# A scan kernel's prologue, written anew in halves of tokens and chunks of channels

## The chip, the cores and the metric

The kernel runs on one core of a Trainium2 chip. A core has five engines that work side by side: TensorE (PE, matrix products), VectorE (DVE), ScalarE (ACT, activation functions), GpSimd (POOL) and SyncE (SP, which here only issues DMA transfers). Each engine takes its own instructions strictly in order; semaphores make one wait for another. The metric is the time on the device in microseconds (us): the median of three runs. The profile is of one further execution.

## The reference, cut to what matters

The input x is 8 batches of 512 tokens by 256 channels, in fp32. Four layers are added to it one after the other: a Mamba block (layer a), a gated recurrence over the batches (layer b), an attention with 16 heads (c), and the recurrence once more (d). All of the change lies in the opening of layer a:

```python
h = layernorm(layernorm0(x), ln1_g, ln1_b)
y = rmsnorm(h, rms_w)
xi, z = split(y @ in_proj_w)                  # 256 channels each
xc = silu(causal_conv4(xi) + conv_b)
dbc = xc @ x_proj_w                           # 64 + 16 + 16 columns
delta = softplus(dbc[..., :64] @ dt_proj_w + dt_proj_b)
Bm, Cm = dbc[..., 64:80], dbc[..., 80:96]
# for every channel and each of 16 states, along the tokens:
#   s = exp(delta * A) * s + delta * xc * Bm ;  y = sum(s * Cm)
...
h = h + ((y + D * xc) * silu(z)) @ out_proj_w
x = x + h ; x = x + ffn(layernorm(x))
```

## The kernel before, in words

**Tiling.** 512 tokens by 256 channels are held either with tokens on the 128 partitions (4 token chunks of 256 channels, TC) or with channels on the partitions (2 channel chunks, KC, of 512 tokens). The scan works on 32 units for each batch; a unit is 8 channels times 16 states, 128 rows of 512 tokens, and two units make a pair, so a batch has 16 pairs. Units 0 to 15 are channel chunk 0, and units 16 to 31 chunk 1.

**The way of a batch to the scan** (`mamba_in`). Layer norm: `stats` on DVE and POOL (the power -0.5 runs on POOL, L82), `center` on ACT (L108), `affine` (L186, L187), `square` on ACT (L193, each with a read of its accumulator), `rms`, `outer` (ACT) and `residual` (the part that is added back later, L204), `scale` (ACT, L208). Then `turn` (PE, transposes) and `turn_` (ACT), `proj` (PE), `proj_` (ACT) and `conv` (DVE, L243), the two Silu pieces, `xproj` (PE) and its copy `xproj_` (ACT), which also stores the B and C rows to DRAM; `dt` (PE) and `dt_` (ACT), and the softplus: `soft_exp` (Exp and two Identity on ACT), `soft_rest` (two subtractions), `soft_ln` (Ln on ACT), `soft` (two DVE operations that give dl, which is delta, and dx, which is delta times xc). `side` is DVE for batch 0 and POOL for the others: it runs `affine`, `residual` and `soft_rest`. Last, `store_dl` and `store_dx` write dl and dx to DRAM, 512 KB each.

**The scan loop.** A unit's rows of dl and dx are loaded back from DRAM by SP, each row to 16 partitions (`load_unit`, L361, 256 KB each). `decay` is an Exp on ACT from dl into one of three PSUM tiles (L368), `increments` a product on POOL for each pair (bx, L375), and `scan_pair` runs two scans (L384) and two products (L388) on DVE. The tiles of loaded rows are pairs, three for dx and three for dl, so dx of pair 3 is loaded when the increments of pair 0 have been made.

**The order.** All of it is written out by hand: `manual_schedule` keeps each engine's instructions in the order of the program. `FRONT` is the list that runs first. In it `i` is batch 0 and `e` is batch 1, whose opening pieces (`stats` to `square`) also belong to the front. Behind FRONT stand the loads of the first pairs in one loop over the units 0 to 7 (dx of all eight, dl of the first six), the increments of pairs 0 and 1, and the decays of units 0 to 2. Then come 16 slots for each batch (`SLOTS`): in slot n the scan of pair n, decays, increments and loads ahead of it, and between them pieces of the next batch (`i`), of the one after that (`e`) and of the one before (`o`, `r`, `q`). The first two slots begin

```python
da0 y a.take_c bx i.rms i.scale scan q.g0 o.gate1 i.turn1 i.turn0 ld q.i0_ q.g0_ i.turn1_ da1 i.turn0_
da0 scan q.update0 da1 ld o.proj0 o.proj1 i.proj0 bx
```

where `i` is by now batch 1 (its `rms` waits for its `square`, which is in the front), `bx` makes the increments of the pair two ahead, `da0` and `da1` the decays of the third and fourth unit after the pair's first, and `ld` loads dx four pairs ahead and dl three ahead.

**PSUM.** Products and transposes of `mamba_in` use three tiles with the tag "mm" in turn; one is free again when its last reader has run.

Of the kernel before, what the change touches and what calls it, by code (L numbers as in the profile page):

```python
# [9 lines left out]
F32 = mybir.dt.float32  # L10
# [5 lines left out]
P = 128  # L16
B = 8
L = 512
# [6 lines left out]
QR = 4  # L25
KCONV = 4
# [35 lines left out]
def token_stats(cx, x, name):  # L62

    nc = cx.nc
    st = cx.small.tile([P, TC, 6], F32, tag="st", name=f"st_{name}")
    mv = cx.small.tile([P, TC, 2], F32, tag="mv", name=f"mv_{name}")
    for c in range(TC):
        nc.vector.bn_stats(st[:, c, :], x[:, c, :])
    for c in range(TC):
        nc.vector.bn_aggr(mv[:, c, :], st[:, c, :])  # L70
    return mv


def inv_sqrt(cx, v, scales, name):

    nc = cx.nc
    n = len(scales)
    ve = cx.small.tile([P, n, TC], F32, tag=f"ve{n}", name=f"ve_{name}")
    r = cx.small.tile([P, n, TC], F32, tag=f"rs{n}", name=f"rs_{name}")
    for i, (scale, eps) in enumerate(scales):  # L80
        nc.vector.tensor_scalar(ve[:, i, :], v, scale, eps, ALU.mult, ALU.add)  # L81
    nc.gpsimd.tensor_tensor(  # L82
        r.rearrange("p n c -> p (n c)"),
        ve.rearrange("p n c -> p (n c)"),
        cx.neg_half[:, : n * TC],
        ALU.pow,
    )
    return r


def layernorm_scales(cx, x, name, scales=((1.0, EPS),)):

    nc = cx.nc
    mv = token_stats(cx, x, name)
    neg = cx.small.tile([P, TC], F32, tag="neg", name=f"neg_{name}")
    nc.vector.tensor_scalar_mul(neg, mv[:, :, 0], -1.0)
    r = inv_sqrt(cx, mv[:, :, 1], scales, name)
    nb = cx.small.tile([P, len(scales), TC], F32, tag=f"nb{len(scales)}", name=f"nb_{name}")
    for i in range(len(scales)):
        nc.gpsimd.tensor_mul(nb[:, i, :], neg, r[:, i, :])  # L100
    return [(r[:, i, :], nb[:, i, :]) for i in range(len(scales))]


def normalize(cx, out, x, scales):

    r, nb = scales
    for c in range(TC):
# [5 lines left out]
def to_channels(cx, src, k, tag, name, bufs=None):  # L113

    ps = cx.psum.tile([P, L], F32, tag=tag, name=name, bufs=bufs)
    for c in range(TC):
        cx.nc.tensor.transpose(ps[:, ts(c, P)], src[:, c, ts(k, P)], cx.ident)  # L117
    return ps

# [48 lines left out]
def mamba_in(cx, a, t, b):  # L168
# [12 lines left out]
    def center():  # L181
        t.h = cx.tok.tile([P, TC, E], F32, tag="hh", bufs=1, name=f"h_{n}")
        normalize(cx, t.h, t.x, t.inner)

    def affine():
        side.tensor_mul(t.h, t.h, cx.rows3["ln1_g"])  # L186
        side.tensor_add(t.h, t.h, cx.rows3["ln1_b"])  # L187

    def square():
        t.ms = cx.small.tile([P, TC], F32, tag="ms", name=f"ms_{n}")  # L190
        sq = cx.ch.tile([P, E], F32, tag="sq", bufs=1, name=f"sq_{n}")
        for c in range(TC):
            nc.scalar.activation(sq, t.h[:, c, :], AF.Square, accum_out=t.ms[:, c : c + 1])  # L193
# [12 lines left out]
    def scale():  # L206
        for c in range(TC):
            nc.scalar.activation(  # L208
                t.h[:, c, :], t.h[:, c, :], AF.Copy, scale=t.rms[:, 0, c : c + 1]
            )  # L210
        t.hT = cx.ch.tile([P, KC, L], F32, tag="T", bufs=3, name=f"hT_{n}")
# [91 lines left out]
    def soft_exp():  # L303

        t.w = cx.tok.tile([P, KC, L], F32, tag="h", name=f"w_{n}")
        nc.scalar.activation(t.e, t.e, AF.Exp, scale=-1.0)
        nc.scalar.activation(t.w, t.e, AF.Identity, bias=cx.one)
        nc.scalar.activation(t.w, t.w, AF.Identity, bias=cx.minus)

    def soft_rest():  # L310
        side.tensor_sub(t.e, t.w, t.e)
        side.tensor_sub(t.dl, t.dl, t.e)

    def soft_ln():
        nc.scalar.activation(t.w, t.w, AF.Ln, bias=cx.one)

    def soft():
        nc.vector.tensor_add(t.dl, t.dl, t.w)
        t.dx = cx.ch.tile([P, KC, L], F32, tag="dx", bufs=1, name=f"dx_{n}")
        nc.vector.tensor_mul(t.dx, t.dl, t.xc)  # L320

    def store(what):
        d = cx.dram.tile([KC, P, L], F32, tag=what, name=f"{what}_dram_{n}")
        nc.sync.dma_start(d.rearrange("k p l -> p k l"), getattr(t, what))
        setattr(t, what + "_d", d)
# [3 lines left out]
        for f in (  # L329
            stats, center, affine, square, rms, outer, residual, scale, silu_z, silu_x, xproj,  # L330
            xproj_, rows, take_c, soft_exp, soft_rest, soft_ln, soft,
        )
    }
    for what in ("dl", "dx"):
        pieces[f"store_{what}"] = lambda what=what: store(what)
# [44 lines left out]
def scan_pair(cx, t, b, pair):  # L380
    units = (2 * pair, 2 * pair + 1)
    for u in units:
        t.hc[u] = cx.scan.tile([P, L], F32, tag="hc", bufs=8, name=f"hc_a{b}_{u}")
# [22 lines left out]
def mamba_out(cx, a, t, b):  # L406
# [26 lines left out]
    def add_proj():  # L433
        for c0, ps in t.proj.items():
            nc.vector.tensor_add(t.u[:, c0 : c0 + 2, :], t.u[:, c0 : c0 + 2, :], ps)
# [4 lines left out]
    def residual():  # L440
        nc.gpsimd.tensor_add(t.x, t.x, t.u)

    def stats():
        t.scales = layernorm_scales(cx, t.u, n)

    def norm():
        t.un = cx.tok.tile([P, TC, E], F32, tag="h", name=f"un_{n}")
        normalize(cx, t.un, t.u, t.scales[0])
        t.h2 = cx.ch.tile([P, KC, L], F32, tag="T", bufs=3, name=f"h2_{n}")

    def turn(k):
        t.ps["h2", k] = to_channels(cx, t.un, k, "mm", f"ps_h2_{n}_{k}")

    def turn_(k):
        nc.scalar.activation(
            t.h2[:, k, :],
            t.ps["h2", k],
# [48 lines left out]
    t.proj, t.down = {}, {}  # L506
    pieces = {f.__name__: f for f in (add_proj, bias, residual, stats, norm)}
# [934 lines left out]
```

## Time and profile before

| what | value |
|---|---|
| median of 3 runs | 1666.32 us (1663.48 to 1667.64) |
| the profiled execution | 1665.1 us, its span 1663.3 us |
| mean granted TensorE clock | 0.944 of full speed |
| busy share of the span | PE 89%, DVE 70%, ACT 53%, POOL 32% |
| first scan starts | 69.91 us |
| first DVE instruction of the loops of batches 1, 2, 3 (L301) | 151.90, 235.60, 323.34 us |
| loaded rows (dx, dl), 256 KB each | 256 and 256 transfers, median 6.4 us from issue to landing |
| store of dx of batch 0, 512 KB | issued 59.02, landed 2.89 us later |

The span is from the first instruction to the last; the execution's own time has 1.8 us more around it. A line of the profile gives a start, a length, the engine, the line of the kernel, the operation, its tiles (with buffer numbers left out) and, in brackets, how long the engine had been idle before it and what released it. "x4" merges four instructions. SPq and ACTq are DMA issues on these queues. An ACT_TABLE_LOAD brings in the table of another activation function.

### The profile page before, as it was taken

What the parts mean: (1) busy time and instruction counts of PE and PEld (TensorE: products, weight loads), DVE (VectorE), ACT (ScalarE), POOL (GpSimd) and SP (SyncE); (2) the same over time, 40 slices, a digit from 0 to 9 for tenths busy, and PEclk for the clock granted to TensorE, in tenths of its full rate; (3) what the DMA queues carried; (4) which work ended last, traced back from release to release, by engine and by line L of the source; (5) the groups of instructions that cost most, each with busy time, mean ns of one, the idle gap of its engine ahead of it and who ended that gap; (6) DMA issues with size and microseconds to landing.
All of it is one profiled execution on the core that took longest, in us unless ns stands there. A gap on an engine that the chain in (4) does not pass through costs nothing.

```text
span 1663.3 us, 19592 instructions
## 1 busy us (share of the span) xinstructions
PE 1487.2 (89%) x6756; PEld 700.3 (42%) x6756; DVE 1169.9 (70%) x1643; ACT 884.3 (53%) x1323; POOL 529.9 (32%) x307
## 2 busy tenths in 40 slices
PE   2155989999999999998878999999999999999998
PEld 1012544546464646465542333333333333333346
DVE  3398998999989898972136777666676667665435
ACT  4465867677777766542223545454544545454522
POOL 3358685858686765633100000000000000000000
PEclk9575999999999999998988999999999999999999
DMA  5697988797979797950210111101010110100023
GB/s 191 160 251 205 248 214 216 219 245 210 260 207 250 198 241 200 256 128 13 67 51 25 33 27 30 34 27 33 18 39 21 38 26 26 26 8 25 28 93 126
DMA packets 110403, 196.02 MB, mean 118 GB/s; under 512 B 16448, under 2 KB 25984, under 8 KB 110304
## 3 DMA queue, kind: packets, MB, share of 16 engines
q1 hardware_dynamic: 107648, 186.61, 43.1%
q10 hardware_dynamic: 1824, 5.15, 0.9%
q0 software_dynamic: 832, 3.02, 0.5%
q8 instruction: 53, 0.87, 0.2%
q14 instruction: 46, 0.38, 0.1%
HBM read 159.06 MB, written 23.07 MB: 109 GB/s over the span
## 4 chain that ended last, share of the span: by engine, by line
PE 67%; DVE 19%; ACT 5%; DMA 4%; issue 3%; POOL 2%; SPq 1%; DVEq 0%; ACTq 0%; POOLq 0%
PE ps_s_c L1014 10%; PE ps_e_c L1014 9%; DVE hc_a L384 8%; PE ps_o_c L1060 8%; PE ps_f_o L470 5%; PE ps_f_o L494 4%; DVE hc_a L388 3%; PE ps_in_a L225 2%; PE ps_v_c L988 2%; PE ps_w_c L1101 2%; PE ps_f_d L543 2%; PE ps_i_d L543 2%; PE ps_g_d L543 2%; PE ps_f_d L552 2%; PE y_a L397 2%
## 5 line engine op out<-in xcount | busy, mean ns | idle before, releaser
L1025 DVE TENSOR_REDUCE mp<-ps_s_c 128x2 f32<-128x1024 f32 x256 | 301.9, 1221 | 183.0 <-PE ps_s_c L1014 182.6
L375 POOL TENSOR_TENSOR bx_a<-dx_rep_a,B_a 128x1024 f32<-128x1024 f32 x128 | 301.9, 2369 | 117.0 <-DVE hc_a L384 54.6
L1051 ACT ACTIVATE e_c<-ps_e_c 128x1024 f32<-128x1024 f32 x256 | 248.9, 1021 | 155.2 <-PE ps_e_c L1014 152.3
L384 DVE TENSOR_TENSOR_SCAN hc_a<-da_a,bx_a 128x512 f32<-128x512 f32 x256 | 298.5, 1206 | 18.9 <-POOL bx_a L375 11.3
L368 ACT ACTIVATE da_a<-dl_rep_a,neg_a 128x512 f32<-128x512 f32 x256 | 173.5, 688 | 135.7 <-DVE hc_a L384 91.7
L1014 PE MATMUL ps_s_c<-keys,q_c 32*128 32x512 f32 x1024 | 184.1, 646 | 2.2 <-ACT e_c L1051 1.7
L1014 PE MATMUL ps_e_c<-q_c,keys 32*128 32x512 f32 x1024 | 169.1, 644 | 3.7 <-DVE mp L1025 3.7
L388 DVE TENSOR_TENSOR hc_a<-hc_a,Cp_a 128x512 f32<-128x512 f32 x256 | 161.0, 669 | 0.0
L1060 PE MATMUL ps_o_c<-e_c,va 128*32 128x512 f32 x1024 | 138.9, 608 | 0.4 <-ACT oT_c L1076 0.3
L470 PE MATMUL ps_f_o<-h_o,w 128*128 128x256 f32 x512 | 121.7, 388 | 0.4 <-ACT f_o L483 0.4
L494 PE MATMUL ps_f_o<-w,f_o 128*128 128x256 f32 x512 | 114.2, 381 | 3.9 <-ACT f_o L483 3.9
L82 POOL TENSOR_TENSOR rs_d<-ve_d,neg_half 128x4 f32<-128x4 f32 x8 | 8.1, 1016 | 342.2 <-DVE ve_d L81 342.2
L397 PE MATMUL y_a<-hc_a,sum 128*32 128x512 f32 x512 | 92.0, 699 | 23.9 <-DVE hc_a L388 15.5
L470 PEld LDWEIGHTS ps_f_o<-h_o,w 128*128 128x128 f32 x512 | 97.3, 193 | 35.2 <-issue 12.2
L494 PEld LDWEIGHTS ps_f_o<-w,f_o 128*128 128x128 f32 x512 | 96.4, 190 | 23.1 <-ACT f_o L483 5.6
L82 POOL TENSOR_TENSOR rs_c<-ve_c,neg_half 128x4 f32<-128x4 f32 x8 | 8.1, 1014 | 301.5 <-DVE ve_c L81 301.5
L1014 PEld LDWEIGHTS ps_s_c<-keys,q_c 32*128 32x128 f32 x1024 | 59.0, 184 | 99.7 <-issue 38.5
L1014 PEld LDWEIGHTS ps_e_c<-q_c,keys 32*128 32x128 f32 x1024 | 51.6, 185 | 101.2 <-issue 67.3
L483 ACT ACTIVATE f_o<-ps_f_o,vecs 128x256 f32<-128x256 f32 x128 | 52.5, 469 | 33.7 <-PE ps_f_o L470 30.9
L117 PE MATMUL ps_hT_a<-ident,h_a 128*128 128x128 f32 x64 | 12.8, 339 | 63.1 <-ACT h_a L208 63.1
L225 PE MATMUL ps_in_a<-hT_a,w_in 128*128 128x512 f32 x128 | 68.1, 671 | 1.1 <-ACT hT_a L220 1.1
L1060 PEld LDWEIGHTS ps_o_c<-e_c,va 128*32 128x32 f32 x1024 | 20.4, 108 | 92.4 <-issue 82.6
(220 smaller groups left out, 2154.5 us busy)
## 6 DMA issues: line engine op xcount, KB each, us to landing
dx_rep_a<-dx_dram_a SPq DMA_DIRECT2D x256, 256.0 KB, 6.4
dl_rep_a<-dl_dram_a SPq DMA_DIRECT2D x256, 256.0 KB, 6.4
x<-in_x_dram SPq DMA_DIRECT2D x8, 512.0 KB, 9.2
dl_dram_a<-dl_a SPq DMA_DIRECT2D x8, 512.0 KB, 6.1
dx_dram_a<-dx_a SPq DMA_DIRECT2D x8, 512.0 KB, 3.1
pre_dram_b<-pre_b ACTq DMA_DIRECT2D x8, 512.0 KB, 5.1
pre_back<-pre_dram_b SPq DMA_DIRECT2D x8, 512.0 KB, 3.3
keys<-xT_c SPq DMA_DIRECT2D x128, 32.0 KB, 1.9
```

Source lines behind the costliest of these rows:

```text
L225: nc.tensor.matmul(ps, a.in_proj[:, k, ts(m, P)], t.hT[:, k, :], start=(k == 0), stop=(k == KC - 1))
L368: cx.nc.scalar.activation(t.da[u], t.dl_rep[u // 2][:, u % 2, :], AF.Exp, scale=a.A[:, u : u + 1])
L375: cx.nc.gpsimd.tensor_mul(t.bx[pair], t.dx_rep[pair], t.B.unsqueeze(1).to_broadcast([P, 2, L]))
L384: cx.nc.vector.tensor_tensor_scan(t.hc[u], t.da[u], t.bx[pair][:, u % 2, :], 0.0, ALU.mult, ALU.add)
L388: cx.nc.vector.tensor_mul(t.hc[u], t.hc[u], t.Cp)
L397: cx.nc.tensor.matmul(t.y[k][head(j), :], a.sum[:, r, :], t.hc[4 * quad + j], start=(r == 0), stop=(r == QR - 1),)
L470: nc.tensor.matmul(ps[:, m, :], a.w1[:, k, ts(m0 + m, P)], t.h2[:, k, ts(half, L // 2)], start=(k == 0), stop=(k == KC - 1),)
L494: nc.tensor.matmul(ps, t.f[:, m, ts(c % 2, P)], a.w2[:, m, :], start=(m == 0), stop=(m == FC - 1),)
L1014: cx.nc.tensor.matmul(ps[:, i, :], lhs[rows, :], rhs[rows, :], start=True, stop=True)
L1025: cx.nc.vector.tensor_reduce(c.mp[:, t, h : h + 2, DH], ps, AX.X, ALU.max, negate=True)
L1051: cx.nc.scalar.activation(e, ps, AF.Exp)
L1060: cx.nc.tensor.matmul(po[head(j), :], c.va[b % 2][:, t, g * HG + j, :], es[j // 2][:, j % 2, :], start=(t == 0), stop=(t == TC - 1),)
```

## The change

The pieces are cut. `center`, `affine`, `square` and `scale` can be had in halves of the tokens (".a" is token chunks 0 and 1, ".b" 2 and 3), and `silu_x`, `soft_exp`, `soft_rest`, `soft_ln`, `soft`, `store_dl` and `store_dx` in chunks of the channels (".0", ".1"). Each stays available whole, and the slots of the loop, which are not changed, use it whole, so batches 1 to 7 run the instructions that they ran. The front uses the cut pieces for batch 0 (`i`), and the loads, increments and decays of the first pairs become part of its list: `dl0` loads both units of pair 0, `bx0` makes its increments, `da0` is the decay of unit 0. The number of rows loaded is the same. e.stats stands behind i.rms, e.outer and e.center at other places, silu_z and proj2, proj3 near the end.

```diff
+    def center(half):
+        if not half:
+            t.h = cx.tok.tile([P, TC, E], F32, tag="hh", bufs=1, name=f"h_{n}")
+        cs = part_of(half)[2]
+        r, nb = t.inner
+        normalize(cx, t.h[:, cs, :], t.x[:, cs, :], (r[:, cs], nb[:, cs]))
...
+    def silu_xk(k):
+        nc.scalar.activation(t.xc[:, k, :], t.xc[:, k, :], AF.Silu)
+
+    def soft_exp(k):
+
+        if not k:
+            t.w = cx.tok.tile([P, KC, L], F32, tag="h", name=f"w_{n}")
+        e, w = (x[:, chunk(k), :] for x in (t.e, t.w))
+        nc.scalar.activation(e, e, AF.Exp, scale=-1.0)
+        nc.scalar.activation(w, e, AF.Identity, bias=cx.one)
+        nc.scalar.activation(w, w, AF.Identity, bias=cx.minus)
...
+    def soft(k):
+        if not k:
+            t.dx = cx.ch.tile([P, KC, L], F32, tag="dx", bufs=1, name=f"dx_{n}")
+        dl, w, dx, xc = (x[:, chunk(k), :] for x in (t.dl, t.w, t.dx, t.xc))
+        nc.vector.tensor_add(dl, dl, w)
+        nc.vector.tensor_mul(dx, dl, xc)
+
+    def store(what, k):
+        if not k:
+            d = cx.dram.tile([KC, P, L], F32, tag=what, name=f"{what}_dram_{n}")
+            setattr(t, what + "_d", d)
+        to, x = (
+            y[:, chunk(k), :]
+            for y in (getattr(t, what + "_d").rearrange("k p l -> p k l"), getattr(t, what))
+        )
+        nc.sync.dma_start(to, x)
...
 FRONT = """
-i.stats e.stats i.center i.affine i.square i.outer i.rms i.residual i.scale i.turn0 i.turn0_
-i.turn1 i.turn1_ i.proj0 i.proj0_ i.proj1 i.proj1_ i.conv0 i.conv1 e.center e.outer i.proj2 i.proj3
-i.silu_z i.silu_x i.xproj i.xproj_ e.affine i.dt0 i.dt0_ i.dt1 i.dt1_ i.rows i.soft_exp i.soft_rest
-i.soft_ln i.soft i.store_dl i.store_dx e.square e.residual
+i.stats i.center.a i.center.b i.outer i.affine.a i.affine.b i.square.a i.square.b i.residual i.rms
+e.stats i.scale.a i.scale.b i.turn0 i.turn1 i.turn0_ i.turn1_ i.proj0 i.proj0_ i.proj1 i.conv0
+i.proj1_ i.silu_x.0 i.conv1 i.silu_x.1 i.xproj e.center i.xproj_ i.dt0 i.dt0_ i.soft_exp.0
+i.soft_rest.0 i.soft_ln.0 e.outer i.soft.0 i.dt1 i.rows i.store_dl.0 i.dt1_ i.soft_exp.1
+i.store_dx.0 dl0 i.proj3 i.proj2 e.affine dx0 i.soft_rest.1 e.residual i.soft_ln.1 dl1 i.soft.1 da0
+dx1 dx2 e.square bx0 i.store_dl.1 da1 i.silu_z bx1 dl2 da2 i.store_dx.1 dx3
 """
...
     for one in FRONT.split():
-        piece(-1, one)
-    for u in range(8):
-        for what in ("dx", "dl"):
-            if what == "dx" or u < 6:
+        what, n = one[:-1], int(one[-1]) if one[-1].isdigit() else None
+        if "." in one:
+            piece(-1, one)
+        elif what == "bx":
+            increments(cx, T[0], 0, n)
+        elif what == "da":
+            decay(cx, a, T[0], 0, n)
+        else:
+            for u in (2 * n, 2 * n + 1):
                 load_unit(cx, T[0], 0, u, what)
-    for pair in range(2):
-        increments(cx, T[0], 0, pair)
-    for u in range(3):
-        decay(cx, a, T[0], 0, u)
```

The recurrence (`recurrent_step`) and the output pieces of `mamba_out` are also written so that they could be had in halves, but are only used whole (`for half in (None,)`), with the instructions that they had.

## The prediction, made before the run

> **What bounds the kernel now.** First the page's slices, 41.6 us each: VectorE (DVE), TensorE's granted clock and the share of the DMA engines.
>
> ```profile
> DVE  3398998999989898972136777666676667665435
> ...
> PEclk9575999999999999998988999999999999999999
> DMA  5697988797979797950210111101010110100023
> ```
>
> From the third slice to the seventeenth DVE is busy throughout: the scan loop, eight batches. Only the first two slices are thin, and the change is there. Second, the chain that ended last, cut to 0 to 160 us (start, length, what):
>
> ```profile
> 1.77 12.90 DMA x<-in_x_dram
> ...
> 17.87 1.14 DVE h_a L186
> ...
> 22.51 1.97 ACT u_a L108 x4
> 24.50 1.24 DVE u_a L204
> ...
> 59.02 2.89 DMA dx_dram_a<-dx_a
> ...
> 78.66 1.03 POOL rs_a_r L82
> 79.71 0.52 ACT h_a L208
> ...
> 84.47 7.25 DMA dl_rep_a<-dl_dram_a
> 91.76 0.04 issue
> 91.81 0.69 ACT da_a L368
> 92.50 0.70 ACT xc_a L232
> ```
>
> See where it leaves batch 0's own work: it goes through batch 1's x (landed 14.67, needed only by e.stats), through `outer` and `residual` ahead of `scale`, and at 84.47 through the replicated loads. Third, the order of time at the points I measure from:
>
> ```profile
> 25.82 1.71 ACT L208 ACTIVATE h_a<-h_a,rs_a_r 128x256 f32<-128x256 f32 x4 [1.35 <-DVE u_a L204]
> ...
> 49.18 1.28 ACT L306 ACT_TABLE_LOAD   x1
> 50.47 1.06 ACT L306 ACTIVATE e_a<-e_a 128x1024 f32<-128x1024 f32 x1
> ...
> 69.91 2.34 DVE L384 TENSOR_TENSOR_SCAN hc_a<-da_a,bx_a 128x512 f32<-128x512 f32 x2 [10.24 <-POOL bx_a L375]
> ...
> 83.36 2.34 DVE L384 TENSOR_TENSOR_SCAN hc_a<-da_a,bx_a 128x512 f32<-128x512 f32 x2 [5.36 <-ACT da_a L368]
> ```
>
> The first scan starts at 69.91, the third pair at 83.36; from 83.36 to the first instruction of batch 1's loop (151.90) DVE idles only some 5 us. So what is gained in front of the loop moves all that follows, unless a queue in the ramp takes some back. Nothing later hangs on the clock on the wall: the weights and x of batches 0 to 4 are in by about 27 us.
>
> **The change, part by part.** The code for batches 1 to 7 runs the same instructions in the same order; only the front differs. I follow it in absolute time.
>
> *To scale.* `center` starts at 9.96 as before; its two halves and `outer` follow on ACT (2.07 and 2.06) to 14.0. DVE meanwhile does `affine` in four half pieces. The 128x1024 one takes 1.22; for half I take 0.65, between 0.61 (half of it) and 0.67 (the 128x512 multiply L388). From 11.1 they end at 13.7, so they are hidden under `outer`. e.stats, which had held `affine` until 17.79, now stands behind i.rms. The four `square` with their accumulator reads take 2.13 (20.38 to 22.51), so to 16.1; ve 0.2 and pow 1.0 with the handovers give `scale` at 17.4, against 25.82: **8.4 gained**. The `residual` (1.23) runs from 14.0 and is off the path. The four L159 reductions (1.24) belong to no list; wherever they fall between 7.7 and 24 DVE has room.
>
> *To the first stores.* From scale on I keep the trace's distances: proj0_ 5.95 after it (23.35), conv0 ending at 26.45, conv1 at 28.7. The Silu table load lies under conv0; silu_x.0 is done at 27.8, silu_x.1 at 29.4. (Before, e.center, e.outer, silu_z and a joint silu_x stood on ACT from 34.17 to 41.55.) xproj's first half runs under conv1, its second (1.66, at the slow clock of the trace, 0.61) under e.center, which is 2.06 on ACT to 31.45. Then xproj_ 0.58, dt0 and its handover 1.22, dt0_ 1.27: 34.5. Table load 1.29. Exp and two Identity on 128x512 cost 2.15: the 128x1024 rows are 1.06 and 1.15, the half rows lie near 0.69 (L368). Load 1.29, Ln 0.73: 40.0, with soft_rest.0 (1.3) beneath the load. soft.0 adds 0.65: store_dl.0 is issued at 40.7, store_dx.0 at 41.4. A store of 512 KB landed in 2.89, the 64 KB one in 1.6; 256 KB lies between, I take 2.2. So the first replicated load is issued at 42.95, against 61.93: **19.0 gained**.
>
> *The ACT queue after that.* e.outer 2.06, dt1_ 1.27, load 1.29, exp.1 2.15, load 1.29, ln.1 0.73, load 1.29, da0 0.7, e.square 2.16, da1 0.7, load 1.29, silu_z 1.09, load 1.29, da2 and da3 0.7 each: from 40.0 to 58.7. There are eight table loads where there were four. i.rms of batch 1 now waits on DVE for e.square (52.95), and the first scan is queued behind it: 53.2, against 69.91 (16.7 gained). Pair 1 waits for da2: 58.05, against 74.48 (16.4).
>
> *The replicated loads.* Before, the first landed 3.4 after its issue, at 65.3, and the 25th (dl of unit 10, the one in the chain) at 91.72: 1.10 each, an unbroken stream of 256 KB. Now the first lands at 46.35 and the tenth (dx2) at 56.25. bx0 and bx1 (2.35 each) run from 49.7 and 54.1, bx2 from 56.45 to 58.8; batch 1's pow, queued behind it on POOL, is done at 59.85. ACT is free at 58.7, so POOL sets batch 1's `scale`: 59.9. Pair 2 began 3.65 after scale, so 63.5, against 83.36: 19.9 gained. Then the stream takes over: up to dl of unit 10 there are the same 24 intervals (26.5) and the two chunk-1 stores between them. A store's share of the stream no row shows alone; it is over nothing and at most a load's 1.10, I take 0.65. 46.35 + 26.5 + 1.3 = 74.2, against 91.72: **17.5 gained**. SP's waits don't starve the stream: dx3 waits for bx0 (52), dx4 for bx1 (56.5), dx6 for bx3 (about 64), each with several loads outstanding. da of unit 10 stands before proj1_, then come conv1 and pair 4 (3.74 later): 77.9 for 95.46. From there on DVE is full, and 17.5 stays.
>
> Unknowns: if the DRAM tile is tracked whole, store_dl.1 waits for dl0 and dl1 to land (about 52), and store_dx.1 for dx2 (56.3); the stream gets a hole worth 1.4 in all; if by chunk, 0. proj2 and proj3 hold two PSUM buffers until silu_z (56.0), before the transposes at 60 want them: 0; were silu_z over 4 late, scale's transposes would be late by the rest. e.affine (4.7) and e.residual on POOL end at about 44.5, 5 before bx0. POOL's bx0 overlaps soft.1 on DVE by 1; a DVE add beside POOL is seen at 2.55 instead of 1.23 (L318), so at most 1.3 on chunk 1, which has slack.
>
> **A rule against it.** The new order switches between Exp, Ln and Silu four more times. The row: a load starts at 49.18, the Exp behind it at 50.47, so a switch is 1.29. The Trainium skill, "ScalarE: Activation LUTs", section "What ACT_TABLE_LOAD costs", gives about 1.28 for the load plus 1.38 of drain, 2.66 per switch, and its section on table sets says to batch by set. By the rule seven loads on the way to da3 would each be 1.37 longer, 9.6 in all: scale at 68.3, pair 2 at 71.9, **11.5** gained. I take the row, since the wait ahead of the Exp shows no drain, and keep 11.5 for the range.
>
> **The sum.** The profiled execution took 1665.1 (span 1663.3): 1665.1 - 17.5 = 1647.6. The median shown is 1.2 above it: **1649**.
>
> **The rivals.**
> 1. *The loads don't bind* and pair 2's 19.9 stays: 1646.4. For: DVE waited only 0.7 for proj1_ at 93.23, so a little slack frees it. Against: DMA is at its limit between 60 and 100 us.
> 2. *Less arrives* (dear switches, a hole in the stream, half-size pieces dearer than taken): about 11.5 gained, 1655. For: ACT has no gap from 33 to 58. Against: the load rows.
> 3. *The loop gives it back*: no change, 1666. Against: nothing behind the front has a fixed date.
> 4. *Slower.* In the loop DVE waits for the Ln on ACT (L315) each batch, 3.96 and 3.88 us in the first two. If the new phase between ACT and DVE on entry made it longer in every batch, 8 batches at 4 more are 32: 1649 + 32 = 1681; it decides from 2.2 per batch. For: ACT comes in late. Against: the order within the loop is untouched, and the batches repeat within 83.7 to 87.7 from the copy L301 to the next.
>
> **How the numbers follow.** The forecast itself (15.5 to 19.5 gained) 0.50, rival 1 0.20, rival 2 0.20, rival 3 0.03, rival 4 0.07. This kernel's measurement can tell about 0.3%, 5 us, from no change. Faster 0.90, same 0.03, slower 0.07. The forecast's own range is 1647 to 1651; with rival 1 (down to 23 gained) and rival 2 (up to 10 gained) it is 1643 to 1657, leaving out rivals 3 and 4 and the tails.
>
> **What would show it.** After: `scale` of batch 0 near 17.4; the first store near 40.7; eight table loads of 1.28 before the first loop; the first scan near 53, pair 2 near 63.5, pair 4 near 78; the copy L301 of batch 1 near 134; periods as before. I am wrong if switches show 2.7 from end to start, if pair 4 comes after 84 with earlier dates kept (stream), or if L301's periods grow.

## The result, and the profile after

The changed kernel takes **1647.88 us** (median of 4 runs, 1642.94 to 1649.03), and the kernel before, measured beside it, 1666.59 us (4 runs, 1663.48 to 1667.64). The ratio is 0.9885, with a 95% interval of 0.9861 to 0.9909: faster by 18.7 us. The profiled executions took 1647.11 and 1665.1 us, 18.0 apart.

The page's slices of the kernel after, 41.1 us each, one digit for each:

```profile
span 1645.3 us, 19612 instructions
...
DVE  3699998989899989951156777675675767656435
...
PEclk8656989999999999999988999999999999999999
DMA  6989897989989787920211111101010110100123
```

The second slice of VectorE (DVE) went from 3 to 6 tenths. From the third to the seventeenth the row is as full as it was, so the gain lies in front of the scan loop.

The chain that ended last, of the kernel after (start, length, what), from batch 0's scale to the fifth pair of scans:

```profile
16.89 0.52 ACT h_a L221
...
32.06 2.09 PE ps_dt_a L298 x2
...
54.17 1.28 ACT L269
...
57.86 0.32 ACT da_a L408
58.18 7.01 DMA dl_rep_a<-dl_dram_a
...
65.27 0.56 ACT da_a L408
65.83 7.76 DMA dl_rep_a<-dl_dram_a
...
73.68 0.69 ACT da_a L408
74.37 0.71 ACT xc_a L247
75.10 0.76 DVE xc_a L258
...
77.34 2.34 DVE hc_a L424 x2
```

Batch 1's x and `residual` are gone from it; `outer` still lies in it, on ACT ahead of `square`. It runs through batch 0's own work, then from 34 to 58 us through ScalarE (ACT) almost without a gap, and from 58.18 through two replicated loads. The second of these is dl of unit 10. It landed at 73.60, and the decay of unit 10 at 73.68 is followed by proj1_ of batch 1 (74.37, L247), its conv (L258) and the fifth pair. In the kernel before the same link stood at 84.47 to 92.50.

The order of time in the kernel after (start, length, engine, line, operation, tiles, and in brackets the idle time before it with what ended it):

```profile
16.89 1.71 ACT L221 ACTIVATE h_a<-h_a,rs_a_r 128x256 f32<-128x256 f32 x4 [1.33 <-POOL rs_a_r L84]
...
26.54 1.28 ACT L319 ACT_TABLE_LOAD   x1 [0.71 <-DVE xc_a L258]
27.83 0.63 ACT L319 ACTIVATE xc_a<-xc_a 128x512 f32<-128x512 f32 x1
...
34.17 0.69 ACT L303 ACTIVATE dl_a<-ps_dt_a,vecs 128x512 f32<-128x512 f32 x1 [2.16 <-PE ps_dt_a L298]
...
41.67 0.35 SPq L354 DMA_DIRECT2D dl_dram_a<-dl_a  x1
43.72 1.18 SPq L401 DMA_DIRECT2D dl_rep_a<-dl_dram_a  x2
...
53.68 2.33 DVE L424 TENSOR_TENSOR_SCAN hc_a<-da_a,bx_a 128x512 f32<-128x512 f32 x2
...
63.85 2.34 DVE L424 TENSOR_TENSOR_SCAN hc_a<-da_a,bx_a 128x512 f32<-128x512 f32 x2 [1.69 <-ACT da_a L408]
...
110.79 2.54 DVE L343 TENSOR_TENSOR dl_a<-dl_a,w_a 128x1024 f32<-128x1024 f32 x1 [3.96 <-ACT w_a L337]
...
133.76 0.69 DVE L316 COPY Cp_a<-C_a 128x512 f32<-128x512 f32 x1
```

Batch 0's scale starts at 16.89 (25.82 before), the first scan at 53.68 (69.91), the third pair, which the prediction calls pair 2, at 63.85 (83.36), the fifth pair at 77.34 (95.46), and the copy that opens batch 1's loop at 133.76 (151.90). So 18.1 us are won at the fifth pair and 18.1 at batch 1's loop. The copies of the later batches stay 16.2 to 17.6 earlier (the last of them 651.20 against 668.74), and layer b's first product into ps_cu_b starts at 828.92 against 846.87, 17.95 earlier. DVE's wait for the Ln of batch 1 is 3.96, as it was; in the kernel before:

```profile
95.46 2.33 DVE L384 TENSOR_TENSOR_SCAN hc_a<-da_a,bx_a 128x512 f32<-128x512 f32 x2
...
128.91 2.55 DVE L318 TENSOR_TENSOR dl_a<-dl_a,w_a 128x1024 f32<-128x1024 f32 x1 [3.96 <-ACT w_a L315]
```

Nothing is given back.

### The profile page after: what moved, and what is told of

Its sections match the earlier page's. It is cut to its first block, busy times and chain, and to the rows that moved or that the text cites. A ratio compares the mean times of both kernels' runs of the same rounds, so it can differ in the third digit from the quotient of the medians.

```text
span 1645.3 us, 19612 instructions
## 1 busy us (share of the span) xinstructions
PE 1489.6 (91%) x6756; PEld 700.2 (43%) x6756; DVE 1171.5 (71%) x1649; ACT 890.8 (54%) x1332; POOL 529.9 (32%) x307
## 4 chain that ended last, share of the span: by engine, by line
PE 68%; DVE 18%; ACT 5%; DMA 4%; issue 3%; POOL 2%; SPq 0%; DVEq 0%; ACTq 0%; POOLq 0%
PE ps_s_c L1079 10%; PE ps_e_c L1079 9%; DVE hc_a L424 8%; PE ps_o_c L1125 8%; PE ps_f_o L518 6%; PE ps_f_o L542 5%; DMA dl_rep_a<-dl_dram_a 4%; DVE hc_a L428 4%; PE ps_v_c L1053 2%; PE ps_w_c L1166 2%; PE ps_f_d L595 2%; PE ps_i_d L595 2%; PE ps_f_d L604 2%; PE ps_g_d L595 2%; PE y_a L437 2%
## 5 line engine op out<-in xcount | busy, mean ns | idle before, releaser
L415 POOL TENSOR_TENSOR bx_a<-dx_rep_a,B_a 128x1024 f32<-128x1024 f32 x128 | 302.4, 2374 | 98.4 <-DVE hc_a L424 55.4
L552 DVE TENSOR_TENSOR x<-x,ps_f_o 128x256 f32<-128x256 f32 x32 | 13.4, 417 | 61.3 <-PE ps_f_o L542 61.0
```

Of the source, the lines that this page charges most:

```text
L415: cx.nc.gpsimd.tensor_mul(t.bx[pair], t.dx_rep[pair], t.B.unsqueeze(1).to_broadcast([P, 2, L]))
```

## The experiments

Five theories stand in the expectations. **S**: what the fifth pair waits for is the stream of replicated loads, through the decay of unit 10, which stands in ACT's queue ahead of proj1_ of batch 1. **Rival 1**: the loads don't bind, and batch 1's scale sets the fifth pair. **Rival 2**: ACT's table loads set it. **Rival 3**: the loop gives it back. **Rival 4**: the loop's wait for the Ln grows. The last expectation adds a **Rival 5**. All edits are made on the kernel after. "Fifth pair" is the start of its two scans; since the inputs land at slightly different times in each execution, I also give it from the issue of the first store. In the kernel after that is 77.34 - 41.67 = 35.67.

### Each half of the change alone

The first kernel has the halves of tokens up to `scale` and then the old order, whole pieces and all loads behind. The second has whole pieces up to `scale` and then the new order.

```diff
 i.stats i.center.a i.center.b i.outer i.affine.a i.affine.b i.square.a i.square.b i.residual i.rms
-e.stats i.scale.a i.scale.b i.turn0 i.turn1 i.turn0_ i.turn1_ i.proj0 i.proj0_ i.proj1 i.conv0
-i.proj1_ i.silu_x.0 i.conv1 i.silu_x.1 i.xproj e.center i.xproj_ i.dt0 i.dt0_ i.soft_exp.0
...
+e.stats i.scale.a i.scale.b i.turn0 i.turn0_
+i.turn1 i.turn1_ i.proj0 i.proj0_ i.proj1 i.proj1_ i.conv0 i.conv1 e.center e.outer i.proj2 i.proj3
+i.silu_z i.silu_x i.xproj i.xproj_ e.affine i.dt0 i.dt0_ i.dt1 i.dt1_ i.rows i.soft_exp i.soft_rest
+i.soft_ln i.soft i.store_dl i.store_dx e.square e.residual
+old
...
+        if one == "old":
+            for u in range(8):
...
```

> The new list up to scale.b (halves of tokens, e.stats behind i.rms), and from the first transpose on the old list with the whole pieces and the old loop of loads. Theory S (whatever brings the first replicated load forward moves all that follows by as much): scale starts at 16.9 as in the changed kernel, so everything behind it comes 8.9 us earlier than in the kernel before: dl stored near 48.9, first load 53.0, third pair of scans 74.4, fifth pair 86.5, time 1657.7. Rival (the two parts share one limit): this part alone gives less than 5 us, 1662 or more.

```diff
-i.stats i.center.a i.center.b i.outer i.affine.a i.affine.b i.square.a i.square.b i.residual i.rms
-e.stats i.scale.a i.scale.b i.turn0 i.turn1 i.turn0_ i.turn1_ i.proj0 i.proj0_ i.proj1 i.conv0
+i.stats e.stats i.center i.affine i.square i.outer i.rms i.residual i.scale
+i.turn0 i.turn1 i.turn0_ i.turn1_ i.proj0 i.proj0_ i.proj1 i.conv0
```

> The old list up to scale, and from the first transpose on the new one (chunks of channels, loads between them). Theory S: scale at 25.8 as before, then the new kernel's distances: first chunk of dl stored near 50.6, first load 52.6, fifth pair of scans 86.3, time 1656.8; the gains of the two halves of the change (8.9 and 9.8) add up to the whole. Rival (one limit shared): this part alone gives nearly the whole 18, or nearly nothing.

The halves of tokens alone take 1657.19 us (ratio 0.9952, 0.9936 to 0.9967), 7.8 less than before; the first store was issued at 50.48 and the fifth pair began at 86.32. The chunks of channels alone take 1655.84 (0.9942, 0.9925 to 0.9958), 9.2 less (both against 1665.02, the kernel before beside them); first store at 49.63, fifth pair at 85.40. Both came within a microsecond of the expected time (1657.7 and 1656.8). Together the two save 17.0 us by their medians, where the whole change saves 18.7. By the copy that opens batch 1's loop they are 9.15 and 10.07 earlier, 19.2 together, against 18.14. The two sums miss the whole on different sides, so within what single executions scatter **the parts add**.

### proj1_ ahead of the decay of unit 10

If the loads bind only because a decay that waits for one stands ahead of proj1_, exchanging the two must free the fifth pair.

```diff
+            if b == 0 and slot == 3:
+                text = text.replace("da1 i.proj1_", "i.proj1_ da1")
             for one in text.split():
```

> The changed kernel, but in slot 3 of batch 0 alone ACT takes batch 1's proj1_ ahead of the decay of unit 10. Theory S (the stream of replicated loads binds, through the decay of unit 10 that stands in front of proj1_): proj1_ no longer waits for the load that lands at 73.6, VectorE's 2.08 us wait before the second conv goes, the fifth pair starts at 75.3 instead of 77.34, time 1645.8. Rival 1 (the loads do not bind): fifth pair at 77.3, time as the changed kernel's, 1647.9.

1644.52 us (0.9875, 0.986 to 0.9889). In the order of time of this kernel:

```profile
64.77 2.34 DVE L424 TENSOR_TENSOR_SCAN hc_a<-da_a,bx_a 128x512 f32<-128x512 f32 x2 [2.22 <-ACT da_a L408]
...
73.06 0.78 ACT L247 ACTIVATE xc_a<-ps_in_a,vecs 128x512 f32<-128x512 f32 x1 [1.00 <-PE ps_in_a L240]
...
74.54 0.69 ACT L408 ACTIVATE da_a<-dl_rep_a,neg_a 128x512 f32<-128x512 f32 x1 [0.69 <-DMA dl_rep_a<-dl_dram_a]
...
76.11 2.33 DVE L424 TENSOR_TENSOR_SCAN hc_a<-da_a,bx_a 128x512 f32<-128x512 f32 x2
```

proj1_ now waits for TensorE (PE) and not for a load; the decay behind it still waits for one. The fifth pair comes 34.05 after the first store (42.06) instead of 35.67: 1.6 earlier. From the third pair (64.77) to the fifth it is 11.34 us, of which DVE idles for 0.14, where the kernel after takes 13.49 and idles for 2.22. So the load did bind, by 2.1 us from the third pair on; counted from the first store 1.6 are left, because batch 1's scale came 0.5 later here (19.07 after the store instead of 18.54). Right behind the load binds what the prediction's rival 1 named: batch 1's scale, the third pair 3.65 behind it, and then DVE, which is full. By the medians the two kernels are not told apart for certain: this one lies 3.4 lower, and 3.2 lower than the kernel after run a second time (below), but the intervals overlap, with the second by only 0.0007.

### More loads in the stream

Loads that nobody reads go to free tiles, in the queue behind dl2: first two, then six, of 256 KB each, replicated like the others.

```diff
-dx1 dx2 e.square bx0 i.store_dl.1 da1 i.silu_z bx1 dl2 da2 i.store_dx.1 dx3
+dx1 dx2 e.square bx0 i.store_dl.1 da1 i.silu_z bx1 dl2 extra da2 i.store_dx.1 dx3
...
+        if one == "extra":
+            x = cx.ch.tile([P, KC, L], F32, tag="T", bufs=3, name="extra")
+            for u in range(2):
+                nc.sync.dma_start(x[:, u, :], T[0].dl_d[0, u * CG : (u + 1) * CG, :].unsqueeze(0).to_broadcast([NS, CG, L]))
```

> The changed kernel with two more replicated loads of 256 KB, issued after dl2 into an idle tile that nothing reads. Theory S (stream): two more at 1.10 each, the dl rows of unit 10 land 2.2 us later (75.8), fifth pair at 79.5, time 1650.1. Rival 1 (the loads do not bind): fifth pair within 0.5 us of 77.3 and the time unchanged.

1648.29 us (0.9903, 0.9886 to 0.992). The fifth pair came at 78.05, 35.97 after the first store: only 0.3 later than in the kernel after, which looks like Rival 1. But the stream was faster in this execution, 282 GB/s from 64 to 68 us where the kernel after had 250. From 48 to the landing of unit 10 at 74.31 it moved 0.66 MB more than the kernel after did in those 26.3 us, which is two and a half loads. **Inconclusive** against the kernel after, and the reason for six. (Another run speaks for S: the kernel with the idle products, below, has no added loads and a stream of 284 GB/s. There the fifth pair came 34.03 after the first store, 1.9 before this one.)

> As with two more loads, but six (256 KB each, into tiles that lie idle then and that nothing reads). With two the result told nothing, because in that run the stream moved 282 GB/s where the changed kernel's moved 250. Theory S (stream): at 250 GB/s the rows of unit 10 land 6.3 us later and the fifth pair starts at 83.6, time about 1654; at 282 GB/s the pair starts near 80.5, time 1651. Rival 1 (the loads do not bind): 77.3 and 1647.9 at either rate.

1653.37 us (0.9929, 0.9915 to 0.9944), 5.7 above the kernel after, which was run beside it (1647.69, below). In the order of time of this kernel:

```profile
70.63 0.69 ACT L408 ACTIVATE da_a<-dl_rep_a,neg_a 128x512 f32<-128x512 f32 x1 [5.81 <-DMA dl_rep_a<-dl_dram_a]
...
78.89 0.69 ACT L408 ACTIVATE da_a<-dl_rep_a,neg_a 128x512 f32<-128x512 f32 x1 [2.40 <-DMA dl_rep_a<-dl_dram_a]
...
82.54 2.33 DVE L424 TENSOR_TENSOR_SCAN hc_a<-da_a,bx_a 128x512 f32<-128x512 f32 x2
```

The third pair was untouched (63.73). Then ACT stood idle for 5.81 for a load, the decay of unit 10 started at 78.89, and the fifth pair came at 82.54, 41.36 after the first store: 5.7 later than in the kernel after. The whole time lost 5.7 as well. S holds and Rival 1 falls: **time added to the stream is time of the kernel**, one for one, to the end. Time taken out of it pays only for the 2.1 us found above; then DVE binds.

### The same kernel once more

Is 250 GB/s a property of this kernel? The kernel after was run unchanged with the six loads.

> The changed kernel once more, to see what of the small differences lies in the run: whether the stream's rate (250 to 283 GB/s seen in kernels that have the same loads) and dt0's result after the copy (2.1 or 1.15 us) come out the same. If they belong to the program, 250 GB/s and 2.1 us as before, fifth pair at 35.7 after the first store; if they belong to the execution, at least one of them differs. Time 1646 to 1649 either way.

1647.69 us (0.9896, 0.9882 to 0.9911), the stream at 246 to 250 GB/s, the fifth pair 35.87 after the first store: as in the kernel after. The windows of the kernel after, then of the kernel with the late stores (next), show the two kinds (window, its length, busy us of PE, PE's weight loads, DVE, ACT, POOL with their counts, granted clock, DMA share, GB/s):

```profile
64.00:68.00 4.00, 3.59 (x4) 1.18 (x4) 4.00 (x5) 2.33 (x4) 2.87 (x2) 0.50 1.07 250
68.00:72.00 4.00, 4.00 (x13) 1.09 (x12) 3.96 (x6) 2.16 (x3) 2.37 (x1) 0.68 1.07 250
```

```profile
64.00:68.00 4.00, 3.75 (x8) 1.21 (x9) 4.00 (x5) 2.00 (x4) 2.67 (x2) 0.50 1.07 262
68.00:72.00 4.00, 4.00 (x17) 1.00 (x20) 3.96 (x6) 2.27 (x4) 2.32 (x2) 0.77 1.07 262
```

The DMA share is the same 1.07 (it can pass 1 because packets of one engine overlap in time); the bytes are not. Over the thirteen profiles of changed kernels the stream moved 246 to 253 GB/s from 68 to 72 us in eight, 262 or 263 in two and 283 or 284 in three. The kernel after is two of the eight; the two at 262 are the two whose stores come late; in the three at 283 I found nothing in common that the others lack. What sets the rate stays open, and so does whether it belongs to a program or to an execution.

### The stores of chunk 1 out of the stream

The prediction gave each of the two chunk-1 stores 0.65 us of the stream. Here they are issued in slot 3 of batch 0, when the loads that matter have been issued.

```diff
-dx1 dx2 e.square bx0 i.store_dl.1 da1 i.silu_z bx1 dl2 da2 i.store_dx.1 dx3
+dx1 dx2 e.square bx0 da1 i.silu_z bx1 dl2 da2 dx3
...
+            if b == 0 and slot == 3:
+                parts["i", -1]["store_dl.1"]()
+                parts["i", -1]["store_dx.1"]()
```

> The changed kernel with the two stores of channel chunk 1 (256 KB each) issued after slot 3 of batch 0 instead of between the first loads; they are needed from unit 16 on. This measures what two stores cost in the stream of loads. Forecast's value 0.65 each: the rows of unit 10 land 1.3 us earlier (72.3), fifth pair at 76.0, time 1646.6. If the stores cost the stream nothing: 73.6, 77.3, 1647.9. At a load's price (1.10 each): 2.2 earlier.

1647.26 us (0.9889, 0.9872 to 0.9905). The fifth pair came at 75.35, 34.42 after the first store, 1.25 earlier than in the kernel after, just the 1.3 that was expected. But the stream ran at 262 GB/s here, and 24 loads at 1.00 instead of 1.05 us are 1.2 by themselves, while three loads that landed late (1.67, 1.23 and 1.76 behind the one before) took 1.5 back. So the hit is luck and doesn't settle the stores' price.

The landings of the kernel after do. The last load ahead of the first store landed at 56.70 and the first load behind the second at 61.01; in these 4.31 us two stores and three loads landed, and the twelve loads that follow landed 1.05 apart. That leaves 1.16 for the two stores. In the ten profiles that have them inside the stream the same sum gives 1.06 to 1.16, at every rate of the stream. The bytes agree: from 52 to 60 us the kernel after moved 256 and 313 GB/s instead of 250, 0.28 MB on top in 8 us; the rest of the stores' 0.52 MB, 0.25 MB, is 1.0 us at 250. So the two cost 1.1 together, a little less than the 1.3 of the prediction.

### Table loads: one earlier, two more

An idle activation on one column of a small tile, with the function Silu, stands ahead of silu_x.0, so that its table can come in while the conv runs.

```diff
-i.proj1_ i.silu_x.0 i.conv1 i.silu_x.1 i.xproj e.center i.xproj_ i.dt0 i.dt0_ i.soft_exp.0
+i.proj1_ Silu i.silu_x.0 i.conv1 i.silu_x.1 i.xproj e.center i.xproj_ i.dt0 i.dt0_ i.soft_exp.0
...
+        if one in ("Silu", "Exp"):
+            tab = cx.small.tile([P, 1], F32, tag="tab", name="tab")
+            nc.scalar.activation(tab, cx.one, getattr(AF, one))
```

> The changed kernel with a Silu on one column of a small tile right behind proj1_ of batch 0, so that the Silu table is loaded before ACT comes to the instruction that waits for the first conv. In the changed kernel that load began only when the conv had ended (26.54). Theory: a table load stands behind the wait of the instruction that it belongs to; taken out of it, the first Silu starts 0.7 us after conv's end less what the tiny Silu costs, xproj and all behind it 0.7 to 1.2 earlier, the first store near 41.0, fifth pair near 76.6. Rival (e.center on ACT hides it): first store unchanged at 41.7.

1646.59 us (0.9882, 0.9867 to 0.9897). In its order of time:

```profile
25.95 1.28 ACT L872 ACT_TABLE_LOAD   x1
...
27.35 0.61 ACT L319 ACTIVATE xc_a<-xc_a 128x512 f32<-128x512 f32 x1
```

proj0_ had begun at 23.44 here and at 23.33 in the kernel after, where the load came at 26.54 and the Silu at 27.83. Measured from proj0_ the load moved ahead by 0.7 and the Silu by 0.6. Yet the first store stood at 41.87 (41.67 after): e.center ran on ACT until 31.6, and xproj_ had to wait for that in both. The rival was right: nothing gained.

The other experiment sets two idle activations, Exp and Silu, behind silu_z, so that two more tables are loaded ahead of da2.

```diff
-dx1 dx2 e.square bx0 i.store_dl.1 da1 i.silu_z bx1 dl2 da2 i.store_dx.1 dx3
+dx1 dx2 e.square bx0 i.store_dl.1 da1 i.silu_z Exp Silu bx1 dl2 da2 i.store_dx.1 dx3
```

> The changed kernel with two more table switches (an Exp and a Silu on one column) right behind silu_z, ahead of the decay of unit 2: about 3.0 us more on ACT. Theory S (stream): the second pair 3.0 later (61.6), batch 1's scale 2.0 later (62.2, since it had waited 1.05 for POOL), third pair near 65.8, but the fifth pair still at 77.3 and the time unchanged. Rival 2 (ACT's switches set what the change brings): fifth pair at 80.3, time 1650.9. If a switch costs 2.66, the second pair is 5.7 later.

1647.03 us (0.9886, 0.9871 to 0.99). In its order of time, the second and the fifth pair:

```profile
62.03 2.34 DVE L424 TENSOR_TENSOR_SCAN hc_a<-da_a,bx_a 128x512 f32<-128x512 f32 x2 [4.47 <-ACT da_a L408]
...
78.25 2.33 DVE L424 TENSOR_TENSOR_SCAN hc_a<-da_a,bx_a 128x512 f32<-128x512 f32 x2
```

With the first store at 42.05, 0.38 later than in the kernel after, the second pair is 3.0 later than there (58.65), batch 1's scale 1.9 later and the fifth pair only 0.5. The time is the same. Rival 2 falls: two switches of 1.3 with their idle activations cost ACT 3.0 us, and the stream hides all but 0.5 of it.

### Idle products to keep PE awake

In the kernel after dt0's product came 2.16 us after the copy that it waits for, where the prediction took 1.22, and the granted clock was 0.60 and 0.50 around it. Three products that nobody reads are set behind proj1.

```diff
-e.stats i.scale.a i.scale.b i.turn0 i.turn1 i.turn0_ i.turn1_ i.proj0 i.proj0_ i.proj1 i.conv0
+e.stats i.scale.a i.scale.b i.turn0 i.turn1 i.turn0_ i.turn1_ i.proj0 i.proj0_ i.proj1 warm i.conv0
...
+        elif one == "warm":
+            ps = cx.psum.tile([P, L], F32, tag="y", bufs=1, name="ps_warm")
+            for i in range(3):
+                nc.tensor.matmul(ps, a.in_proj[:, 0, ts(i, P)], T[0].hT[:, 0, :], start=True, stop=True)
```

> The changed kernel with three products that nothing reads (128x512, into the idle bank of y) between proj1 and xproj on TensorE, so that it does not stand idle from 25 to 28.5 us. Theory: the granted clock had fallen there, and that is why dt0's result came 2.1 us after the copy instead of 1.15; with the gap filled dt0 takes 1.15 again, the first store comes about 1.0 earlier (40.7), fifth pair at 76.3, time 1646.9. Rival (not the clock): dt0 stays at 2.1 and nothing moves.

1646.41 us (0.9882, 0.9868 to 0.9897). In its order of time:

```profile
33.77 0.69 ACT L303 ACTIVATE dl_a<-ps_dt_a,vecs 128x512 f32<-128x512 f32 x1 [1.21 <-PE ps_dt_a L298]
```

The clock was 1.00 from 29 to 32 us and 0.83 from 32 to 35, against 0.60 and 0.50 in the kernel after, and dt0 took 1.21. The first store was 35.68 after the first statistics of x instead of 36.57. But the kernel with the late stores and the one with six more loads had 1.21 as well, without idle products. So the 0.95 us go with the clock that PE is granted in that execution; that the products secure it is not shown. The fifth pair came at 75.31, 34.03 after the first store, 1.0 before the expectation: at this execution's 284 GB/s the row of unit 10 landed at 70.98, and DVE idled for only 0.14 of the 11.31 us from the third pair to the fifth, as with proj1_ first.

### The loop's wait for the Ln

At L343 DVE waits 3.96 and 3.88 us for the Ln of batches 1 and 2, 1.75 to 1.84 in the next four, and in the last 1.04 for POOL. Behind the Ln's place in ACT's queue `e.outer` could stand instead of ahead of it.

```diff
-ld scan e.outer i.soft_rest da0 o.up4 i.soft_ln o.add0 c.gate0 o.up5 y bx o.up7 o.up4_ da1 o.up6 o.up5_ e.affine o.up6_
+ld scan i.soft_rest da0 o.up4 i.soft_ln e.outer o.add0 c.gate0 o.up5 y bx o.up7 o.up4_ da1 o.up6 o.up5_ e.affine o.up6_
```

> The changed kernel, with e.outer moved behind i.soft_ln in slot 10 of every batch, so that ACT does the Ln about 2 us earlier. In the loop VectorE waits 3.96 us for it in batch 0. POOL's second subtraction ends 0.85 before the add begins, so the wait can shrink by 0.85 at most: in 7 batches 6 us, time 1642. That would show that the wait which rival 4 named sits on ACT's order. If POOL or what comes behind e.outer (POOL's affine and residual) takes it back: 1647.9 or more.

1647.58 us (0.9899, 0.9882 to 0.9915), a miss. In its order of time:

```profile
110.06 3.35 DVE L343 TENSOR_TENSOR dl_a<-dl_a,w_a 128x1024 f32<-128x1024 f32 x1 [3.15 <-POOL dl_a L333]
```

The Ln was 1.9 earlier, but now the add waits for POOL's subtraction (L333), starts 0.7 earlier and takes 3.35 instead of 2.54, beside POOL's next operation: it ends at 113.4, where it ended at 113.3. The reason is in the end and not in the wait. While the add runs, POOL makes increments (L415), and in all seven batches of both kernels the add ends 1.08 or 1.09 us after they do: at 113.33 after 112.25, here at 113.41 after 112.33. It takes 3.35 or 2.54 according to how early it starts beside them. By these timings the increments set that point of the loop, so the earlier Ln moved nothing.

### The ramp with what was learnt

The idle products, the late stores, proj1_ first, and batch 1's `rms` ahead of bx2 in slot 0, so that POOL's power for batch 1's scale doesn't stand behind increments.

```diff
+            if b == 0 and slot == 3:
+                text = text.replace("da1 i.proj1_", "i.proj1_ da1")
+            if b == 0 and slot == 0:
+                text = text.replace("bx i.rms", "i.rms bx")
             for one in text.split():
...
```

> Four edits of the changed kernel at once, all of them in the stretch from proj1_ of batch 0 to the fifth pair: the three idle products behind proj1 of batch 0, both stores of chunk 1 issued in slot 3 instead of inside the front, batch 1's proj1_ ahead of the decay da1 of slot 3, and batch 1's rms ahead of bx2 in slot 0, so that POOL's power no longer stands behind increments. The chain from the first store to the fifth pair was 35.67 us in the changed kernel and 34.05 with proj1_ ahead alone. S (the stream binds through what stands behind its loads): with proj1_ free of the loads, what is left is ACT's queue and batch 1's scale (ACT free at 59.2, the scale at 60.2); taking POOL's power out of it gives at most 1.0, and the stores nothing more: fifth pair 33.0 to 33.5 after the first store, time 1643.5 with a first store at 41.3. Rival 1 (the stream has no part): the gains are those of the scale alone, 1.0: fifth pair 34.6, time 1645.5. Rival 5 (nothing adds: decays of unit 9 and 10 behind proj1_ now hold the scans of the fifth pair by the loads themselves): 34.0 after the first store as with proj1_ ahead alone, and 1644.5.

1646.43 us (0.9891, 0.9875 to 0.9908; 1643.46 to 1647.75). In the order of time of its profiled execution, which took 1643.46:

```profile
58.08 1.69 ACT L221 ACTIVATE h_a<-h_a,rs_a_r 128x256 f32<-128x256 f32 x4
...
61.71 2.34 DVE L424 TENSOR_TENSOR_SCAN hc_a<-da_a,bx_a 128x512 f32<-128x512 f32 x2 [0.56 <-ACT da_a L408]
...
70.99 0.69 ACT L408 ACTIVATE da_a<-dl_rep_a,neg_a 128x512 f32<-128x512 f32 x1 [0.75 <-DMA dl_rep_a<-dl_dram_a]
...
73.02 2.33 DVE L424 TENSOR_TENSOR_SCAN hc_a<-da_a,bx_a 128x512 f32<-128x512 f32 x2
...
107.35 2.54 DVE L343 TENSOR_TENSOR dl_a<-dl_a,w_a 128x1024 f32<-128x1024 f32 x1 [4.84 <-ACT w_a L337]
```

Batch 1's scale comes 17.4 after the first store (40.66) instead of 18.5, and the fifth pair 32.36 after it instead of 35.67: 3.3 gained there, more than the 2.2 to 2.7 of S and far from Rival 5's 34.0 after the store. The decay of unit 10 (70.99) still waits for its load, but nothing that the fifth pair needs stands behind it any more. The 3.3 are the scale's 1.1 and 2.2 between the third pair and the fifth, which are 11.31 apart instead of 13.49. DVE is busy 3.9 to 4.0 of each 4 us from 64 to 80: from there on the ramp has nothing more to give. But the wait for the Ln grew from 3.96 to 4.84 and 0.9 was lost again in batch 0: the copy of batch 1 came at 130.32, 3.4 earlier than in the kernel after. This execution was 3.7 us shorter than the profiled one of the kernel after, but the median of four is not: the intervals overlap almost wholly. So no kernel here is shown to beat the changed one; the kernel with proj1_ first comes nearest to it. The stream ran at 263 GB/s, and whether that has a part in the 3.3 is open.

## Why the prediction was right

Predicted 1649, measured 1647.88, with 17.5 gained against 18.0 in the profiled executions. Step by step, in us of the profile:

| step | predicted | measured |
|---|---|---|
| scale of batch 0 starts | 17.4 | 16.89 |
| proj0_ | 23.35 | 23.33 |
| silu_x.0 done | 27.8 | 28.46 |
| xproj_ | 31.45 | 31.42 |
| dt0_ after xproj_ ended | 1.22 | 2.16 |
| first store issued | 40.7 | 41.67 |
| first replicated load issued | 42.95 | 43.72 |
| first scan | 53.2 | 53.68 |
| second pair (pair 1) | 58.05 | 58.65 |
| scale of batch 1 | 59.9 | 60.21 |
| third pair (pair 2) | 63.5 | 63.85 |
| first replicated load landed | 46.35 | 47.04 |
| 24 more loads landed, without the stores | 26.5 | 25.4 |
| the two chunk-1 stores | 1.3 | 1.16 |
| dl of unit 10 landed | 74.2 | 73.60 |
| fifth pair (pair 4) | 77.9 | 77.34 |
| copy of batch 1 | 134 | 133.76 |

**To scale.** From the first `center` it took 7.39 us, predicted 7.44. It starts 0.46 earlier than in the kernel before because x's statistics came earlier in this execution (9.50 against 9.96), not by the change: `vecs`, which DVE waits for first, landed at 4.01 against 4.46. This was lost again at the products of proj0, which took 0.5 longer than before at the same granted clock of 1.00; over the kernels run here the stretch from scale to proj0_ scatters from 5.73 to 6.84.

**The Silu table.** The step "the Silu table load lies under conv0" failed: the load came at 26.54, after the conv, behind the wait of its own activation. It made the Silu 0.65 late and cost nothing, since xproj_ had to wait for e.center, which ended at 31.38; the experiment with the early table, where it ended at 31.6, shows that.

**dt0.** Mis-sized by 0.94: the 1.22 came from the trace of before and holds at a granted clock near 1 (1.00 there); at 0.50 it was 2.16. This is nearly the whole lateness of the first store (0.97). In the kernel before:

```profile
46.74 0.69 ACT L288 ACTIVATE dl_a<-ps_dt_a,vecs 128x512 f32<-128x512 f32 x1 [1.21 <-PE ps_dt_a L283]
```

**Table loads.** Eight of 1.28, and 1.29 to 1.30 from the start of a load to that of its activation. The Trainium skill's 2.66 for a switch ("ScalarE: Activation LUTs", "What ACT_TABLE_LOAD costs") is not what this trace shows, and the two added switches cost 3.0 with their two activations, where the page's figure would make it 5.3 without them. The row was the right choice.

**The stream.** The mechanism was right: unit 10, ahead of proj1_, binds (by 2.1 from the third pair on), and six more loads cost 5.7. The term that was mis-sized the other way than dt0 is the interval of a load. The prediction took 1.10 and an unbroken stream, which is the mean of the kernel before from 65.28 to 91.72. But the landings there lie 1.03 to 1.08 apart except two, 1.48 and 1.96, whose cause stays open. The kernel after has no such late ones: its 24 loads took 25.4 instead of 26.5, 1.1 less. The first load was issued 2.05 behind the store instead of 2.25, and the stores took 1.16 instead of 1.3. So 0.97 late at the first store became 0.56 early at the fifth pair, and the hit to a microsecond is in part luck. In part it hides in the difference, too: from the issue of the first load to the landing of unit 10 it is 29.79 before and 29.88 after, because the two stores cost about what the two late landings had.

SP's waits made no hole: store_dl.1 was issued at 50.27 without waiting for the loads of chunk 0 (the last of dl1 landed at 52.31), so the first unknown took its value of 0. But dx3 did not wait for bx0, which had ended at 53.17. By the trace SP issues a transfer of this stream only when the eighth before it has landed: store_dx.1 went out at 52.37 after a landing at 52.31, dx3 at 53.41 after one at 53.34. With that many outstanding the DMA share stayed at 1.04 to 1.09 in every microsecond from 50 to 60.

**The rivals.** The prediction's rival 1 was near: its time of 1646.4 is 1.5 below the measured one, and proj1_ ahead of the decay found its chain 1.6 to 2.1 behind the stream. Its rival 2, less gained, would have needed dear switches or a hole in the stream, and neither was there. Its rival 3 is refuted by the copies of each batch. Rival 4's wait comes seven times and not eight, and within 0.1 it is the same in both kernels, batch for batch (3.96, 3.88, four of 1.75 to 1.84, and 1.04 or 1.05). In the joined kernel it grew by 0.9 once, in batch 0, so the wait can grow, but it didn't in every batch: there the last copy stands at 647.0, 4.2 ahead of the kernel after.

## What to carry to other kernels

Cost a rewritten prologue in absolute time, engine by engine, down to the transfers, and go on until the engine that is full afterwards: what is won ahead of it stays. Ask at each queue which instruction waits for a transfer and what stands behind it; here one decay in front of a bias add tied the kernel to the DMA stream. An interval taken as the mean of a trace may hold single late ones: look at the landings one by one. Before an experiment is read as a gain of 1 us, look whether the same kernel's clock and DMA rate were the same in that execution.

## What the runs showed of the hardware that was not expected

- A table load isn't taken early: it stands behind the wait of the activation that needs it (26.54, right after the conv), unless an earlier activation asks for the table (25.95).
- The same replicated loads stream at 246 to 284 GB/s in different profiles at the same DMA share of 1.05 to 1.08.
- A 64-row product and its handover took 1.21 us at a granted clock of 0.83 to 1.00 and 2.16 at 0.50; which of the two an execution has differs between kernels that run the same instructions there.
- Two 256 KB stores to DRAM between the loads went half on top of the stream: 313 GB/s while they ran, 250 before and behind, and they put the loads off by 1.06 to 1.16 us together, about one load's interval.
- The 128x1024 add on DVE takes 1.23 alone. Beside POOL's increments it takes 2.54 when it starts 0.89 behind them and 3.35 when it starts 0.07 behind them: in both cases it ends 1.08 after them.
